# An edge-gated graph layer on one core: PSUM products copied by ScalarE and used by VectorE two steps later, aggregation in pairs

## The chip, the cores and the metric

The kernel runs on one core of a Trainium2 chip. The metric is the device time of one execution in microseconds. Before the change it is 1182.6 us, the median of three runs (1182.56 to 1185.6). The profiled execution that the tables below come from spans 1195.2 us.

The engines are called as the profile calls them: PE is TensorE (PEld are its weight loads), DVE is VectorE, ACT is ScalarE, POOL is GpSimd, SP is SyncE.

## The reference

There are 16 graphs (batch entries) of 1024 nodes with 256 features, and one sparse matrix `adj` (1024 x 1024) for all of them. For each edge u -> v a gate is computed from the features of both ends, and two sums over the edges go through two weight matrices:

```python
pre_u = einsum('bud,dk->buk', h_t, W1[:d])
pre_v = einsum('bvd,dk->bvk', h_t, W1[d:])
hidden = relu(pre_u[:, :, None, :] + pre_v[:, None, :, :] + b1)
S = sigmoid(einsum('buvk,ko->buvo', hidden, W2)[..., 0] + b2[0])
a_t = einsum('buv,bud->bvd', S * A_a, h_t)
m_t = einsum('uv,bud->bvd', A_m, h_t) * h_t
z_t = beta1 * h_t + beta2 * (einsum('bvd,de->bve', a_t, Wa) + ba) \
                  + beta3 * (einsum('bvd,de->bve', m_t, Wm) + bm)
```

Here `h_t` is `x`, and `A_a` and `A_m` are both `adj`. Some nine entries of a column of `adj` are not zero, so the kernel works on lists of edges.

## The kernel before

The work is cut into 32 blocks: 4 groups of 4 graphs times 8 tiles of 128 nodes v. A block has ten steps (`s` = 0 to 9), two windows of 64 nodes with five tiles of 128 edges each. A step `n` handles one edge tile:

- POOL gathers the tile's rows from a table in HBM by an indirect DMA: per edge 8 KB, namely `pre_u` of four graphs and `h` of four graphs (`fetched`, five buffers).
- PE expands `pre_v` to the edges with a 0/1 matrix (`expand`, into `pc` in PSUM, two buffers).
- VectorE adds the two into `t`, and for each graph does relu, multiplication by `W2` and the sum (`gate`); ScalarE makes the sigmoid `gt` from it and scales the aggregation's left operand `left`.
- PE sums the rows of `h` into the nodes (`aggregate`), in 32-column pieces.

The order of instructions on each engine is the order of the program text (a manual schedule). `after(step, f)` puts `f` into the instruction stream at a later step, in `do(step)`, which stands behind the gate of that step.

```python
def gate(n):
    t = one.tile([P, GB, D], FP, name="t")
    nc.vector.tensor_tensor(t, fetched[n % NF][:, :GD]..., pcs.pop(n)..., ALU.add)          # L539
    for b in range(GB):
        nc.vector.scalar_tensor_tensor(t[:, b, :], t[:, b, :], 0.0, w2_b,
                                       ALU.max, ALU.mult, accum_out=sc[:, b:b + 1])         # L543
    nc.scalar.activation(gt, sc, AF.Sigmoid, bias=b2_b)                                     # L546
    for b in range(GB):
        nc.scalar.activation(lefts[n][:, :m, b, 1, :], lefts[n][:, :m, b, 0, :], AF.Copy,
                             scale=gt[:, b:b + 1])                                          # L549
```

Beside the steps, three jobs of a block are spread over them. `halves` computes `pre_v` of the next block and splits it into a rounded part `X` and the rest `low`[...]. `turn_over` transposes the sums and multiplies one of them by `h`. `block_end` makes the two final products and adds `beta1 * h`:

```python
def halves(k):
    X = cuts[k] = big.tile([P, NW, GD], FR, name="X")
    low = one.tile([P, GD], FR, name="low")
    for h in range(2):
        step = yield
        ...                                                     # pre_v of two graphs, into p (PSUM "misc", two buffers)
        nc.scalar.copy(X[:, 0, c], p)                                                       # L418
        after(step + 1, lambda c=c, p=p: nc.vector.tensor_tensor(
            low[:, c], p, X[:, 0, c].bitcast(FP), ALU.subtract))                            # L419
    ...                                                         # ScalarE moves X and low to where the matmul wants them

def turn_over(k, w, q, step):
    ...                                                         # PE transposes, ScalarE copies into LT (L581)
    def times_h():
        nc.vector.tensor_tensor(m, m, hTs[order[k]]..., ALU.mult)                           # L591
    after(step + 1, times_h)

def block_end(k):
    for h in range(2):
        for bb in range(2):
            step = yield
            if bb == 0:
                pz = small("pz")
                add_row(pz, bias_p)
            for i, wt in enumerate((w_m, w_a)):
                ...                                             # two matmuls each (L608)
        def add(h=h, pz=pz):
            nc.vector.scalar_tensor_tensor(hb[:, 2 * h:2 * h + 2, :], hb[:, 2 * h:2 * h + 2, :], be1,
                                           pz..., ALU.mult, ALU.add)                        # L612
        after(step + 1, add)
    after(step + 2, lambda: nc.sync.dma_start(out[...], hb))
```

The main loop, cut to what matters:

```python
for n in range(total + 2):
    k, s = divmod(n, T)
    if 1 <= n <= total:
        aggregate(n - 1)                                        # L560
        fetch_val(2)
        if n - 1 + NF < total:
            fetch(n - 1 + NF)                                   # L453, into the buffer just used; NF = 5
        if n % TW in (0, MID + 1):
            half_end(n - 1, 0 if n % TW else 1)                 # ScalarE copies a finished sum out of PSUM
    if n < total:
        gate(n)
        ...
    do(n)
    if n + 2 < total:
        expand(n + 2)                                           # L523
    ...                                                         # pieces of halves, turn_over, block_end, tables
```

Blocks of the first two groups run while the tables of the later groups and the edge lists of the later node tiles are still being made (products with `w_u`, transfers of `hT` and `table`, and short VectorE work).

Of the kernel before, what the change touches and what calls it, by code (L numbers as in the profile page):

```python
# [7 lines left out]
FP = mybir.dt.float32  # L8
FR = mybir.dt.float32r
I32 = mybir.dt.int32  # L10
AF = mybir.ActivationFunctionType
ALU = mybir.AluOpType
AX = mybir.AxisListType
P = 128
# [3 lines left out]
def kernel(  # L18
# [42 lines left out]
    nc = tc.nc  # L61
    B, N, D = x.shape
    NT = N // P
    DC = D // P
    GB = 4
    NG = B // GB
    GD = GB * D
# [290 lines left out]
    def after(step, f):  # L358
        due.setdefault(step, []).append(f)
# [48 lines left out]

    def halves(k):
        X = cuts[k] = big.tile([P, NW, GD], FR, name="X")  # L410
        low = one.tile([P, GD], FR, name="low")
        for h in range(2):
            step = yield
            c = slice(2 * h * D, (2 * h + 2) * D)
            p = small("p")
            add_row(p, b1_p)
            half_product(p, hTs[order[k]], w_v, h, True)
            nc.scalar.copy(X[:, 0, c], p)  # L418
            after(step + 1, lambda c=c, p=p: nc.vector.tensor_tensor(  # L419
                low[:, c], p, X[:, 0, c].bitcast(FP), ALU.subtract))  # L420
        yield
        nc.scalar.copy(X[W:, 1, :], X[W:, 0, :].bitcast(FP))
        for w in range(NW):
            yield
            nc.scalar.copy(X[(1 - w) * W:(2 - w) * W, w, :], low[w * W:(w + 1) * W].bitcast(FP))

    engines = mybir.EngineType
    main.enter_context(tc.manual_schedule(
# [80 lines left out]

    marks, pcs, accs, evs, hbs, LTs, lefts = {}, {}, {}, {}, {}, {}, {}

    def load_mark(q):
# [12 lines left out]
    def left_adj(n):  # L527
        k, g, vt, w, j = where(n)
        i = vt * NW + w
        m = len(QUARTERS[j])  # L530
        o = max(2 * j - 1, 0)
        lefts[n] = wk.tile([P, 2, GB, 2, V], FP, name="left")
        nc.scalar.activation(lefts[n][:, :m, :, 0, :], onehot[:, i, o:o + m, :].unsqueeze(2).to_broadcast([P, m, GB, V]),  # L533
                             AF.Copy, scale=val[:, i, j:j + 1])

# [15 lines left out]
    def aggregate(n):  # L551
        k, g, vt, w, j = where(n)
        left, f = lefts.pop(n), fetched[n % NF]
        for i, q in enumerate(QUARTERS[j]):
            h, r = divmod(q, 2)
            first = j == h * MID and r == 0
            if first:
                accs[h] = psa.tile([P, 2, D], FP, name=f"acc{h}")
            for b in range(GB):
                nc.tensor.matmul(accs[h][b * 2 * V:(b + 1) * 2 * V, r, :],  # L560
                                 left[:, i, b].rearrange("p k v -> p (k v)"), f[:, GD + b * D:GD + (b + 1) * D],
                                 start=first, stop=(j == q + 1), skip_group_check=True)


    def half_end(n, q):

        evs[q] = one.tile([P, 2, D], FP, name=f"ev{q}")
        nc.scalar.copy(evs[q], accs.pop(q))  # L568

    def turn_over(k, w, q, step):  # L570
        if w == 0 and q == 0:
            LTs[k] = one.tile([P, DC, GB, 2, P], FP, name="LT")
        LT = LTs[k]
        pt = small("pt")
        ev = evs.pop(q)
        for i in range(4):
            r, c = divmod(i, DC)
            nc.tensor.transpose(pt[:, i * P:(i + 1) * P], ev[:, r, c * P:(c + 1) * P], ident)  # L578
        v = slice(w * W + q * U, w * W + (q + 1) * U)
        r = (w * W + q * U) // V  # L580
        nc.scalar.copy(LT.rearrange("p c b k (r v) -> p r (c b k) v", v=V)[:, r:r + 2],  # L581
                       pt.rearrange("p (r i v) -> p r i v", r=2, v=V))
        apart = k == BS - 1 and w == NW - 1
        if not apart:
            if not q:
                return
            v = slice(w * W, (w + 1) * W)

        def times_h():
            m = LT[:, :, :, 0, v]  # L590
            nc.vector.tensor_tensor(m, m, hTs[order[k]].rearrange("p b c n -> p c b n")[:, :, :, v], ALU.mult)  # L591
            if w == NW - 1 and q == 1:
                del hTs[order[k]]
        after(step + 1, times_h)

    def block_end(k):

        g, vt = order[k]
        hb = hbs[k]
        for h in range(2):  # L600
            for bb in range(2):
                step = yield
                if bb == 0:
                    pz = small("pz")
                    add_row(pz, bias_p)
                for i, wt in enumerate((w_m, w_a)):
                    for c in range(DC):
                        nc.tensor.matmul(pz[:, bb * D:(bb + 1) * D], LTs[k][:, c, 2 * h + bb, i, :], wt[:, c, :],  # L608
                                         start=False, stop=(i == 1 and c == DC - 1), skip_group_check=True)

            def add(h=h, pz=pz):
                nc.vector.scalar_tensor_tensor(hb[:, 2 * h:2 * h + 2, :], hb[:, 2 * h:2 * h + 2, :], be1,  # L612
                                               pz.rearrange("p (b d) -> p b d", b=2), ALU.mult, ALU.add)
            after(step + 1, add)
        after(step + 2, lambda: nc.sync.dma_start(
            out[g * GB:(g + 1) * GB, vt * P:(vt + 1) * P, :].rearrange("b p d -> p b d"), hb))
        del hbs[k], LTs[k]


# [64 lines left out]
    for n in range(total + 2):  # L684
        k, s = divmod(n, T)
        if 1 <= n <= total:
            aggregate(n - 1)
            fetch_val(2)
            if n - 1 + NF < total:
                fetch(n - 1 + NF)  # L690
            if n % TW in (0, MID + 1):
                half_end(n - 1, 0 if n % TW else 1)
        if n < total:
            gate(n)
            if n + 1 < total:
                left_adj(n + 1)
        if n % TW == 1 and n // TW + 1 < total // TW:
            load_mark(n // TW + 1)
# [3 lines that stand above are left out]
        if n == 1:  # L702
            w_a = load_weights(Wa, "w_a", nc.sync)
            w_m = load_weights(Wm, "w_m", nc.sync)
            bias = load_rows(bm, D, "bias", nc.sync)
            ba_b = load_rows(ba, D, "ba_b", nc.sync)
            be1 = load_rows(beta1, 1, "be1", nc.sync)
            be2 = load_rows(beta2, 1, "be2", nc.sync)
            be3 = load_rows(beta3, 1, "be3", nc.sync)
            after(10, scale_late)  # L710
        if s == 4 and k < BS:
            hbs[k] = big.tile([P, GB, D], FP, name="h_blk")
            if k < BS - 1:
                g, vt = order[k]
                nc.sync.dma_start(hbs[k], x_rows[vt * P:(vt + 1) * P, g * GB:(g + 1) * GB, :])
            else:
                for v, m, f in tails:
                    for h, o in tail_rows(x, v, m, f):
                        nc.sync.dma_start(h, o)
        for i in advance.get(n, ()):  # L720
            next(made[i], None)
        if (s == 1 and 0 < k < BS) or n == total:
            turn_over(k - 1, 1, 1, n)
        if s in (3, 4, 5, 6) and 0 < k < BS:
            if s == 3:
                end = block_end(k - 1)
                next(end)
            go(end, n)
        if s == 7 and k < BS:
            turn_over(k, 0, 0, n)  # L730
            turn_over(k, 0, 1, n)
        if s == 9 and k < BS:
            turn_over(k, 1, 0, n)
        if n == total - 2:
            end = tail(tails[:2], n)
            next(end)
        elif n == total - 1:
            go(end, n)
        elif n >= total:
            end = tail([tails[2 + n - total]], n)  # L740
            next(end)
            go(end, n)
            go(end, n)
        if k + 1 < BS and s in (0, 2, 3, 4, 6):
            if s == 0:
                parts = halves(k + 1)
                next(parts)
            go(parts, n)
        if n in loads:
            load_hT(loads[n])  # L750
            if loads[n] not in begun:
                copy_h(loads[n])
                begun.add(loads[n])
        if n in at:
            if at[n] != last:
                last = at[n]
                piece = rows(last)
                next(piece)
            go(piece, n)
        if n == 100:  # L760
            nc.gpsimd.partition_all_reduce(longest, rest, P, bass_isa.ReduceOp.max)
            after(n + 12, count_rest)
# [114 lines left out]
```

## Time and profile before

| | busy, us | share of the span |
|---|---|---|
| PE matmuls | 1097.9 | 92% |
| PE weight loads | 724.7 | 61% |
| VectorE | 1066.9 | 89% |
| ScalarE | 840.4 | 70% |
| GpSimd | 426.1 | 36% |
| DMA | 391.39 MB | mean 327 GB/s |

Shares of a whole span hide that this kernel has stages. How to read on: cut the span where the work changes (here by the starts of the `t` additions, one per step), ask for busy times and DMA share in each stage, then for the waits of the fullest engine there. A row of a wait reads "engine and line that waited <- what ended the wait: us in total, times, longest". A group row reads "line engine operation out<-in, shapes, count | busy us, mean ns of one | idle time before it, and what ended it". Two rows carry most of VectorE's time: the multiply-and-sum L543, 1280 of them at 422 ns, and the addition L539, 320 at 1215 ns.

### The profile page before, as it was taken

What the parts mean: (1) busy time and instruction counts of PE and PEld (TensorE: products, weight loads), DVE (VectorE), ACT (ScalarE), POOL (GpSimd) and SP (SyncE); (2) the same over time, 40 slices, a digit from 0 to 9 for tenths busy, and PEclk for the clock granted to TensorE, in tenths of its full rate; (3) what the DMA queues carried; (4) which work ended last, traced back from release to release, by engine and by line L of the source; (5) the groups of instructions that cost most, each with busy time, mean ns of one, the idle gap of its engine ahead of it and who ended that gap; (6) DMA issues with size and microseconds to landing.
All of it is one profiled execution on the core that took longest, in us unless ns stands there. A gap on an engine that the chain in (4) does not pass through costs nothing. (4 is left out here: it accounts for less than half of the span.)

```text
span 1195.2 us, 23788 instructions
## 1 busy us (share of the span) xinstructions
PE 1097.9 (92%) x7633; PEld 724.7 (61%) x7633; DVE 1066.9 (89%) x3515; ACT 840.4 (70%) x2498; POOL 426.1 (36%) x428
## 2 busy tenths in 40 slices
PE   7667988999889898999999999999999999999986
PEld 6544655666556565666666666666666666666653
DVE  8769879989988988899899999999999999999994
ACT  3346666677667665777777777787878777777873
POOL 1557652433263226333233333333333333333330
PEclk9968899999999999999999999999999999999998
DMA  9988889899979978999999999999999999999992
GB/s 279 312 307 261 258 319 333 315 336 377 320 254 373 361 244 302 357 384 360 351 329 379 359 331 371 362 356 386 358 367 345 356 324 326 326 341 328 335 340 76
DMA packets 147046, 391.39 MB, mean 327 GB/s; under 512 B 16752, under 2 KB 105328, under 8 KB 110704
## 3 DMA queue, kind: packets, MB, share of 16 engines
q0 software_dynamic: 50016, 300.50, 68.5%
q1 hardware_dynamic: 81616, 74.99, 19.6%
q10 hardware_dynamic: 15280, 14.29, 3.7%
q8 instruction: 63, 1.03, 0.3%
q14 instruction: 71, 0.58, 0.1%
HBM read 393.78 MB, written 50.33 MB: 372 GB/s over the span
## 5 line engine op out<-in xcount | busy, mean ns | idle before, releaser
L453 POOL DMA_INDIRECT fetched<-table,uidx x320 | 329.7, 1030 | 675.5 <-PE acc L560 509.6
L543 DVE SCALAR_TENSOR_TENSOR t<-t,w_b 128x256 f32<-128x256 f32 x1280 | 469.3, 422 | 20.1 <-ACT LT L581 0.5
L539 DVE TENSOR_TENSOR t<-fetched,pc 128x1024 f32<-128x1024 f32 x320 | 388.8, 1215 | 22.4 <-DMA fetched<-table,uidx 8.6
L560 PE MATMUL acc<-fetched,left 128*32 128x256 f32 x4096 | 334.2, 394 | 32.3 <-ACT left L549 16.8
L549 ACT ACTIVATE left<-left,gt 128x32 f32<-128x32 f32 (+1 forms) x1280 | 299.4, 304 | 10.4
L523 PE MATMUL pc<-X,mark 128*128 128x512 f32 x640 | 238.1, 454 | 21.1 <-DVE t L539 13.6
L560 PEld LDWEIGHTS acc<-fetched,left 128*32 128x32 f32 x4096 | 129.9, 110 | 177.2 <-issue 46.9
L546 ACT ACTIVATE gt<-sc,b_b 128x4 f32<-128x4 f32 x320 | 95.3, 298 | 140.5 <-DVE t L543 133.9
L523 PEld LDWEIGHTS pc<-X,mark 128*128 128x128 f32 x640 | 97.2, 191 | 156.6 <-issue 102.2
L608 PE MATMUL misc<-w_a,LT 128*128 128x256 f32 x496 | 127.3, 379 | 0.0
L608 PE MATMUL misc<-w_m,LT 128*128 128x256 f32 x496 | 127.1, 378 | 0.0
L384 PE MATMUL misc<-w_u,hT 128*128 128x256 f32 x448 | 109.2, 390 | 11.0 <-ACT few L298 3.6
L533 ACT ACTIVATE left<-onehot,val 128x128 f32<-128x128 bf16 (+1 forms) x320 | 116.5, 364 | 0.0
L384 PE MATMUL misc<-w_v,hT 128*128 128x256 f32 x448 | 107.9, 384 | 0.0
L543 DVE DVE_READ_ACCUMULATOR t<-t,w_b 128x1 f32 x1280 | 104.2, 81 | 0.0
L608 PEld LDWEIGHTS misc<-w_m,LT 128*128 128x128 f32 x496 | 93.7, 189 | 17.2
L384 PEld LDWEIGHTS misc<-w_u,hT 128*128 128x128 f32 x448 | 85.8, 195 | 27.3 <-issue 4.4
L608 PEld LDWEIGHTS misc<-w_a,LT 128*128 128x128 f32 x496 | 94.2, 190 | 12.8
L568 ACT COPY ev<-acc 128x512 f32<-128x512 f32 x128 | 75.1, 587 | 34.7 <-PE acc L560 26.8
L341 POOL DMA_INDIRECT val<-in_adjT_dram,vidx x80 | 83.6, 1046 | 33.4 <-issue 21.9
L384 PEld LDWEIGHTS misc<-w_v,hT 128*128 128x128 f32 x448 | 86.7, 194 | 14.3
L581 ACT COPY LT<-misc 128x512 f32<-128x512 f32 x128 | 71.1, 575 | 24.0 <-PE pc L523 12.0
(158 smaller groups left out, 830.9 us busy)
## 6 DMA issues: line engine op xcount, KB each, us to landing
h_blk<-in_x_dram SPq DMA_DIRECT2D x31, 512.0 KB
out_dram<-h_blk SPq DMA_DIRECT2D x31, 512.0 KB
hT<-in_xT_dram SPq DMA_DIRECT2D x28, 512.0 KB
table<-tab SPq DMA_DIRECT2D x26, 512.0 KB
table<-in_x_dram ACTq DMA_DIRECT2D x24, 512.0 KB
fetched<-table,uidx POOLq DMA_INDIRECT x320
table<-in_x_dram SPq DMA_DIRECT2D x8, 512.0 KB
table<-fetched SPq DMA_DIRECT2D x6, 512.0 KB
```

Source lines behind the costliest of these rows:

```text
L341: nc.gpsimd.indirect_dma_start(out=val[:, i, j:j + 1], out_offset=None, in_=adj_flat, in_offset=bass.IndirectOffsetOnAxis(ap=vidx[:, i, j: ...
L384: nc.tensor.matmul(p[:, bb * D:(bb + 1) * D], hT[:, 2 * h + bb, i, :], wt[:, i, :], start=(i == 0 and not begun), stop=(i == DC - 1), skip ...
L453: nc.gpsimd.indirect_dma_start(out=fetched[n % NF], out_offset=None, in_=table[g], in_offset=bass.IndirectOffsetOnAxis(ap=uidx[:, vt * NW ...
L523: nc.tensor.matmul(pcs[n][:, c], marks[n // TW][:, j * P:(j + 1) * P], cuts[k][:, w, c], start=True, stop=True)
L533: nc.scalar.activation(lefts[n][:, :m, :, 0, :], onehot[:, i, o:o + m, :].unsqueeze(2).to_broadcast([P, m, GB, V]), AF.Copy, scale=val[:, ...
L539: nc.vector.tensor_tensor(t, fetched[n % NF][:, :GD].rearrange("p (b d) -> p b d", b=GB), pcs.pop(n).rearrange("p (b d) -> p b d", b=GB), ...
L543: nc.vector.scalar_tensor_tensor(t[:, b, :], t[:, b, :], 0.0, w2_b, ALU.max, ALU.mult, accum_out=sc[:, b:b + 1])
L546: nc.scalar.activation(gt, sc, AF.Sigmoid, bias=b2_b)
L549: nc.scalar.activation(lefts[n][:, :m, b, 1, :], lefts[n][:, :m, b, 0, :], AF.Copy, scale=gt[:, b:b + 1])
L560: nc.tensor.matmul(accs[h][b * 2 * V:(b + 1) * 2 * V, r, :], left[:, i, b].rearrange("p k v -> p (k v)"), f[:, GD + b * D:GD + (b + 1) * D ...
L568: nc.scalar.copy(evs[q], accs.pop(q))
L608: nc.tensor.matmul(pz[:, bb * D:(bb + 1) * D], LTs[k][:, c, 2 * h + bb, i, :], wt[:, c, :], start=False, stop=(i == 1 and c == DC - 1), sk ...
```

## The change

ScalarE copies what VectorE used to read from PSUM: beside `X` now also the plain product into `low`, and the final product into a new tile `z`. VectorE then works in SBUF, on `low` once per block instead of twice, and one step later than before relative to PE's work. The aim is that VectorE never stands waiting for a product of PE or a copy of ScalarE that is only just being made. `turn_over`'s multiplication is moved one step later too; so that it may be, `block_end` does the product with `w_a` first and the one with `w_m`, which needs the multiplication, a step later. To make room, `h_blk` and `z` have one buffer each, and `h_blk` is loaded in step 0 of the following block.

Aggregation and refill are done in pairs in every even step: two tiles' aggregation one behind the other, each followed by its gather. `left` has four buffers instead of three for that.

```diff
 def halves(k):
-        low = one.tile([P, GD], FR, name="low")
+        low = one.tile([P, GD], FP, name="low")
...
             nc.scalar.copy(X[:, 0, c], p)
-            after(step + 1, lambda c=c, p=p: nc.vector.tensor_tensor(
-                low[:, c], p, X[:, 0, c].bitcast(FP), ALU.subtract))
+            nc.scalar.copy(low[:, c], p)
+        after(step + (2 if k else 1), lambda: nc.vector.tensor_tensor(low, low, X[:, 0, :].bitcast(FP), ALU.subtract))
...
-        lefts[n] = wk.tile([P, 2, GB, 2, V], FP, name="left")
+        lefts[n] = wk.tile([P, 2, GB, 2, V], FP, name="left", bufs=4)
...
-        after(step + 1, times_h)
+        after(step + (1 if k == BS - 1 else 2), times_h)

 def block_end(k):
+        z = big.tile([P, GB, D], FP, name="z", bufs=1)
         for h in range(2):
-            for bb in range(2):
+            for i, wt in ((1, w_a), (0, w_m)):
                 step = yield
-                if bb == 0:
+                if i:
                     pz = small("pz")
                     add_row(pz, bias_p)
-                for i, wt in enumerate((w_m, w_a)):
+                for bb in range(2):
...
-            def add(h=h, pz=pz):
-                nc.vector.scalar_tensor_tensor(hb[:, 2 * h:2 * h + 2, :], hb[:, 2 * h:2 * h + 2, :], be1,
-                                               pz.rearrange("p (b d) -> p b d", b=2), ALU.mult, ALU.add)
-            after(step + 1, add)
-        after(step + 2, lambda: nc.sync.dma_start(... hb))
+            sl = slice(2 * h, 2 * h + 2)
+            nc.scalar.copy(z[:, sl], pz.rearrange("p (b d) -> p b d", b=2))
+            after(step + 2, lambda sl=sl: nc.vector.scalar_tensor_tensor(z[:, sl], hb[:, sl], be1, z[:, sl],
+                                                                         ALU.mult, ALU.add))
+        after(step + 3, lambda: nc.sync.dma_start(... z))
...
         if 1 <= n <= total:
-            aggregate(n - 1)
             fetch_val(2)
-            if n - 1 + NF < total:
-                fetch(n - 1 + NF)
-            if n % TW in (0, MID + 1):
-                half_end(n - 1, 0 if n % TW else 1)
+        if 2 <= n <= total and n % 2 == 0:
+            for i in (n - 2, n - 1):
+                aggregate(i)
+                if i + NF < total:
+                    fetch(i + NF)
+            for i in (n - 2, n - 1):
+                if i % TW in (MID, TW - 1):
+                    half_end(i, 0 if i % TW == MID else 1)
...
-        if s == 4 and k < BS:
-            hbs[k] = big.tile([P, GB, D], FP, name="h_blk")
...                                            # the load of h_blk, and of the last block's rows
+        if s == 0 and 0 < k < BS:
+            hbs[k - 1] = big.tile([P, GB, D], FP, name="h_blk", bufs=1)
+            g, vt = order[k - 1]
+            nc.sync.dma_start(hbs[k - 1], x_rows[vt * P:(vt + 1) * P, g * GB:(g + 1) * GB, :])
+        if n == total - 6:
+            hbs[BS - 1] = hts.tile([P, GB, DC, P], FP, name="hT").rearrange("p b c n -> p b (c n)")
...
-        if k + 1 < BS and s in (0, 2, 3, 4, 6):
+        if k + 1 < BS and s in (0, 2, 3, 5, 6):    # when the pieces of halves are issued
```

More of the change, by code (lines that the diff above doesn't have):

```diff
@@ L424, in halves @@
             yield
-            nc.scalar.copy(X[(1 - w) * W:(2 - w) * W, w, :], low[w * W:(w + 1) * W].bitcast(FP))
+            nc.scalar.copy(X[(1 - w) * W:(2 - w) * W, w, :], low[w * W:(w + 1) * W])
     engines = mybir.EngineType
@@ L599, in block_end @@
         hb = hbs[k]
+        z = big.tile([P, GB, D], FP, name="z", bufs=1)
         for h in range(2):
-            for bb in range(2):
+            for i, wt in ((1, w_a), (0, w_m)):
                 step = yield
-                if bb == 0:
+                if i:
                     pz = small("pz")
                     add_row(pz, bias_p)
-                for i, wt in enumerate((w_m, w_a)):
+                for bb in range(2):
                     for c in range(DC):
                         nc.tensor.matmul(pz[:, bb * D:(bb + 1) * D], LTs[k][:, c, 2 * h + bb, i, :], wt[:, c, :],
-                                         start=False, stop=(i == 1 and c == DC - 1), skip_group_check=True)
-            def add(h=h, pz=pz):
-                nc.vector.scalar_tensor_tensor(hb[:, 2 * h:2 * h + 2, :], hb[:, 2 * h:2 * h + 2, :], be1,
-                                               pz.rearrange("p (b d) -> p b d", b=2), ALU.mult, ALU.add)
-            after(step + 1, add)
-        after(step + 2, lambda: nc.sync.dma_start(
-            out[g * GB:(g + 1) * GB, vt * P:(vt + 1) * P, :].rearrange("b p d -> p b d"), hb))
+                                         start=False, stop=(i == 0 and c == DC - 1), skip_group_check=True)
+            sl = slice(2 * h, 2 * h + 2)
+            nc.scalar.copy(z[:, sl], pz.rearrange("p (b d) -> p b d", b=2))
+            after(step + 2, lambda sl=sl: nc.vector.scalar_tensor_tensor(z[:, sl], hb[:, sl], be1, z[:, sl],
+                                                                         ALU.mult, ALU.add))
+        after(step + 3, lambda: nc.sync.dma_start(
+            out[g * GB:(g + 1) * GB, vt * P:(vt + 1) * P, :].rearrange("b p d -> p b d"), z))
         del hbs[k], LTs[k]
@@ L710 @@
             after(10, scale_late)
-        if s == 4 and k < BS:
-            hbs[k] = big.tile([P, GB, D], FP, name="h_blk")
[L713 to L719, printed above, removed]
+        if s == 0 and 0 < k < BS:
[4 more added lines that the diff above has]
+            hbs[BS - 1] = hts.tile([P, GB, DC, P], FP, name="hT").rearrange("p b c n -> p b (c n)")
+            for v, m, f in tails:
+                for h, o in tail_rows(x, v, m, f):
+                    nc.sync.dma_start(h, o)
         for i in advance.get(n, ()):
```

## The prediction

> **What bounds the kernel now.** I began with the busy row of the page: PE 92%, DVE (VectorE) 89%, DMA mostly 9 tenths in every slice. That average names no bound, so I cut the span into stages. The start of each `t` add (L539, one per step, 320 of them) gives the step times; ten steps are a block. Blocks 0 to 10 take about 39 us each (68 to 500 us), blocks 11 to 22 take 33.0 (500 to 896), and blocks 23 to 31 take 31.1 with hardly any spread (896 to 1177). The windows of the three stages:
>
> ```profile
> core 0: us, PE busy (x) PEld busy (x) DVE busy (x) ACT busy (x) POOL busy (x), PEclk, DMA share, GB/s
> 68.00:500.00 432.00, 387.73 (x2611) 256.45 (x2609) 379.92 (x1266) 289.82 (x859) 188.39 (x186) 0.95 0.89 311
> 500.00:896.00 396.00, 388.07 (x2778) 255.15 (x2774) 364.03 (x1156) 307.18 (x924) 124.50 (x121) 1.00 0.98 361
> 896.00:1177.00 281.00, 268.69 (x1946) 169.76 (x1944) 269.96 (x862) 216.52 (x670) 88.91 (x87) 1.00 0.92 328
> ```
>
> Columns: length, busy time of each engine, granted clock, DMA share, GB/s. Late, VectorE is busy 269.96 of 281 us: it is the bound there. In the middle the DMA engines are at 0.98 while VectorE has 32 us idle; early, nothing is full and VectorE has 52 us idle. So next I asked what VectorE waits for, stage by stage (early, then middle; us in total, times, longest):
>
> ```profile
> DVE low L419 <- ACT X L418: 12.8, 8, 4.4
> DVE h_blk L612 <- PE misc L608: 12.3, 9, 2.7
> DVE LT L591 <- ACT LT L581: 10.9, 7, 3.1
> ...
> DVE h_blk L612 <- PE misc L608: 8.0, 11, 1.3
> DVE t L539 <- DMA fetched<-table,uidx: 6.0, 11, 1.2
> DVE low L419 <- ACT X L418: 5.6, 6, 3.3
> ```
>
> Early 36.0 us and middle 13.6 us of VectorE's waits are at just the three operations that the change delays. Late, the same rows sum to 0.8 us. A third view, the groups of instructions, gives the costs (x count, then busy us, mean ns, idle before):
>
> ```profile
> L539 DVE TENSOR_TENSOR t<-fetched,pc 128x1024 f32<-128x1024 f32 x320 | 388.8, 1215 | 22.4 <-DMA fetched<-table,uidx 8.6 <-PE pc L523 3.4 <-DVE h_blk L612 0.8
> L612 DVE SCALAR_TENSOR_TENSOR h_blk<-h_blk,be,misc 128x512 f32<-128x512 f32 x62 | 46.1, 744 | 20.7 <-PE misc L608 20.6
> L419 DVE TENSOR_TENSOR low<-misc,X 128x512 fp32r<-128x512 f32 x64 | 43.9, 686 | 19.7 <-ACT X L418 19.7
> L591 DVE TENSOR_TENSOR LT<-LT,hT 128x512 f32<-128x512 f32 x55 | 37.8, 688 | 11.1 <-ACT LT L581 10.9
> L418 ACT CAST X<-misc 128x512 fp32r<-128x512 f32 x64 | 37.3, 583 | 38.4 <-PE misc L384 32.4 <-PE pc L523 4.0 <-PE misc L578 1.6
> ```
>
> Last, the refill loop. There are five `fetched` buffers, and POOL issues the next gather only when PE has aggregated the tile, as the waits of the whole run say. The timeline of one middle step shows PE's switch from aggregation to expansion:
>
> ```profile
> POOL fetched L453 <- PE acc L560: 509.6, 220, 6.7
> ...
> 703.18 0.16 PEld L560 LDWEIGHTS acc<-fetched,left 128*32 128x32 f32 x8 [0.17 <-issue]
> 703.18 0.64 PE L560 MATMUL acc<-fetched,left 128*32 128x256 f32 x8
> 703.75 0.30 PEld L523 LDWEIGHTS pc<-X,mark 128*128 128x128 f32 x2 [0.41 <-issue]
> ```
>
> The bracket is idle time: the weight load of `pc` stands 0.41 us after the last narrow load.
>
> From the trace I also took, for each gather, its issue, its landing (the last semaphore update of that DMA) and the add that uses it. Middle, medians: 8.25 us from issue to landing, 1.5 us from landing to use. Late: 7.5 and 2.6. The tightest tile is the one of step 1 of a block: it lands only 0.2 us (middle) and 0.45 us (late) before its add.
>
> [...] L612, which reads PSUM, takes 744 ns and L591, all in SBUF, 688; but L419 reads PSUM too and takes 686. [...] I read PE's 98% in the middle with the 64% of PEld (255.15 of 396) and don't call PE full. [...] gathers slow down while the output and `h_blk` transfers run.
>
> **The change, part by part.**
>
> *VectorE's own work.* A bare step lasts 2.80 us between adds. A late step with a half of `low` is 0.4 to 0.5 us longer (median), one with `h_blk` 0.5 to 0.6. So the two halves cost about 1.0 us per block; one 128x1024 subtraction streams twice the columns of a 512-wide one, so about 1.0 as well (2 x 0.5): nothing gained. The two `h_blk` operations become SBUF only[...]. **Sum: -2 us.**
>
> *VectorE's waits.* `low` runs two steps after ScalarE's second copy instead of one after PE's product, `z` two after its copy, `LT` two after. The longest wait at any of them was 4.4 us and a step is 3.1 to 3.9 us, so nearly all 36.0 + 13.6 us at these rows should be gone. Not all of it comes back as time: in such a pause PE, ScalarE and the DMA queues caught up, and in the middle DMA at 0.98 sets a limit near 33.0 x 0.98 = 32.3 us per block, if its rate stays. I credit 0.65 of the early waits (**-23 us**) and 0.6 of the middle ones (**-8 us**, which is 0.7 us x 12 blocks, just the room that DMA leaves). Late: 0.
>
> *ScalarE.* 64 copies of `low` and 62 of `z`, at the 583 ns of L418: 73 us more on an engine busy 840. In the late stage, 4 per block are 2.3 us on 24 (216.52 / 9 blocks) of 31.1: 26.4, or 85%. The heaviest step, 6, gets 4 left scalings (0.96), the next `left` (0.39), `mark` (0.71), `z` (0.58), the `low` cast (1.04) and the gate's 0.30: 4.0 us against a step of 2.9. It runs 1.1 us late and makes that up by step 8. Beside the path, but with little to spare.
>
> *PE.* The copy out of PSUM now comes from ScalarE within the step, so the two `misc` buffers come free earlier. In pairs the 0.41 us switch occurs 5 times per block, not 10: 2 us per block of weight-load idleness. As PE sets the end in no stage, this only shortens its lag.
>
> *The gathers.* This is the cost. Tile n-1 of a pair is aggregated as before. Tile n-2 was aggregated as soon as its gate was ready; now it stands behind the expansion and the products of the odd step. From PE's order, issue moves from about 5.4 to 6.6 us after use for step 0 (late), 5.8 to 8.5 for step 2, 6.0 to 8.0 for step 4, 6.4 to 7.6 for step 6. The slack of the gathers they start is 2.5, 3.4, 4.0 and 0.45 us. So the late stage has one deficit, at step 1, of about 0.7 us, and in the middle there are two or three of up to 1 us. The output transfer also moves one step later, onto the `h_blk` load: good for step 1, bad for steps 2 and 3. I put it at 0.5 us per block over 21 blocks: **+10 us.**
>
> Sum: -2 -23 -8 +10 = -23, so 1182.6 - 23 = **1160 us**.
>
> **Rivals.** (A) *The wait moves to DMA*: gathers issued late and two at a time leave the queues idle, and VectorE waits at L539 instead. For it: slack under half a microsecond at step 1, and 0.98 DMA share. Against: early slack is 2.5 us and more[...]. With 1.5 us per block over 21 blocks the time would be about 1182. (B) *ScalarE becomes the pace*: `z` and `low` wait in order for PE, then the gate's sigmoid behind them is late, then aggregation and refill. For it: step 6 and the 85%. Against: it already waits 38.4 us for PE at `X` with no harm to VectorE late. With 1 us on 32 blocks: 1190. (C) *The pauses were pure loss*: all 49.6 us come back and DMA keeps up (one block, 500 to 533 us, ran at 382 GB/s). Then 1135.
>
> **Range and chances.** C's 1135 and A's 1182 bracket my sum; I take 1137 to 1188. The 2% line is at 1159, almost my centre, so faster and same are near even. Slower by 2% needs B and A together: 0.05.
>
> **What would show it.** Right: VectorE's waits at `low`, `z` and `LT` under 5 us together; early blocks at 37 us; late blocks within 0.5 us of 31.1; ScalarE's busy time up by 73 us; the wait at L539 for gathers up from 8.6 to 15 or 20 us. The prediction is wrong if that wait passes 30 us, most of it in steps 1 to 3 (A); if VectorE is idle before PE's or ScalarE's rows of the gate chain (B); or if early blocks don't shorten though the waits are gone, which would mean that the pauses lay beside another limit.

## The result and the profile after

The changed kernel takes 1229.95 us (median of four runs, 1225.99 to 1231.27) against 1183.5 us before: ratio 1.0384, 95% interval 1.0354 to 1.0414. It is 46 us slower, and the prediction had said 1160.

The groups of VectorE's instructions, after (busy us, mean ns | idle time before it and what ended it), beside the two new copies on ScalarE:

```profile
L540 DVE TENSOR_TENSOR t<-fetched,pc 128x1024 f32<-128x1024 f32 x320 | 389.5, 1217 | 102.7 <-DMA fetched<-table,uidx 73.5 <-PE pc L524 8.0 <-PE misc L610 4.0
L614 DVE SCALAR_TENSOR_TENSOR z<-h_blk,be,z 128x512 f32<-128x512 f32 x62 | 46.3, 748 | 0.0
L420 DVE TENSOR_TENSOR low<-low,X 128x1024 f32<-128x1024 f32 x32 | 39.0, 1219 | 3.4 <-ACT low L419 3.4
L592 DVE TENSOR_TENSOR LT<-LT,hT 128x512 f32<-128x512 f32 x55 | 37.7, 686 | 0.0
L419 ACT COPY low<-misc 128x512 f32<-128x512 f32 x64 | 37.5, 586 | 0.0
L613 ACT COPY z<-misc 128x512 f32<-128x512 f32 x62 | 36.2, 584 | 31.7 <-PE misc L610 30.9
```

The change did what it was meant to do at the rows it touches: in front of these rows of `z`, `low` and `LT` VectorE is idle for 3.4 us in all, where it was 51.5. But the idle time before the `t` addition is now 102.7 us instead of 22.4, and 73.5 of it ends with the landing of a gather, instead of 8.6.

The windows of the same three stages, with the columns as in the prediction (their ends moved: the blocks 11 to 22 now end at 922 us), and VectorE's waits for gathers in the first two:

```profile
68.00:500.00 432.00, 378.77 (x2599) 263.44 (x2600) 379.36 (x1260) 312.04 (x904) 193.97 (x187) 0.93 0.88 311
500.00:920.00 420.00, 386.36 (x2764) 267.66 (x2763) 363.48 (x1138) 326.83 (x969) 127.72 (x120) 0.97 0.94 340
920.00:1177.00 257.00, 239.49 (x1740) 156.02 (x1738) 241.24 (x761) 211.62 (x635) 85.07 (x80) 1.00 0.89 325
```

```profile
DVE t L540 <- DMA fetched<-table,uidx: 31.5, 19, 5.0
...
DVE t L540 <- DMA fetched<-table,uidx: 36.2, 29, 5.9
```

In the middle the same VectorE work (363.48 us against 364.03) takes 24 us longer, and the DMA share falls from 0.98 to 0.94: the queues have less to do while VectorE waits for them. The experiments below show that this is not a rate limit: the gathers are asked for too late.

Taken by step, 43.7 of the 73.5 us are waited at the additions of step 1, and 67.9 at odd steps. With five buffers the tile of an odd step goes into the buffer of the even tile five steps before it, and the even tiles are those that pairing holds back.

The waits of the whole run show where the request comes from; the last line is the kernel before:

```profile
POOL fetched L453 <- PE acc L561: 547.2, 163, 10.0
PE pc L524 <- DVE t L540: 78.1, 62, 4.6
PE pc L523 <- DVE t L539: 13.6, 14, 2.1
```

POOL waits for PE's aggregation up to 10.0 us at a time (6.7 before). PE in turn stands 78.1 us before its expansion because VectorE hasn't done the addition that frees `pc` (13.6 before). A part of the longest middle block, of 41.7 us, shows the order, from the timeline (start, length, engine, instruction):

```profile
689.75 1.89 PE L384 MATMUL misc<-w_u,hT 128*128 128x256 f32 x8
...
691.28 0.81 PE L524 MATMUL pc<-X,mark 128*128 128x512 f32 x2
...
692.17 1.89 PE L610 MATMUL misc<-w_a,LT 128*128 128x256 f32 x8
...
693.99 1.93 PE L561 MATMUL acc<-fetched,left 128*32 128x256 f32 x32
...
695.37 1.09 POOL L453 DMA_INDIRECT fetched<-table,uidx  x1 [6.95 <-DVE t L540]
...
701.13 1.22 DVE L540 TENSOR_TENSOR t<-fetched,pc 128x1024 f32<-128x1024 f32 x1 [0.94 <-DMA fetched<-table,uidx]
```

The 32 matmuls at 693.99 are a pair: the tiles of steps 2 and 3. VectorE's addition for the first of them was at 683.9 us and the next addition at 686.8, so its gate was done by then. But in PE's queue it stands behind a `w_u` product, an expansion and the `w_a` product; of these the expansion and the `w_a` product (691.28 to 693.99) are what pairing put ahead of it. Its buffer is refilled at 695.37, 11.4 us after its use (the median of the tiles of step 2 in this stage is 10.4), and the gather that this issue starts lands at 701.0, just as VectorE needs it. The bracket of that issue names an addition whose end fell just there; the addition that read this buffer was long done, and what was still missing was the aggregation.

PE's granted clock, a share of its full speed, is lower than before too: 0.97 in the middle stage, where it was 1.00, and 0.88 in this block. In experiments 1 and 14, which don't hold the tiles back, it is 0.99 and 1.00 there. What the slower clock adds to the 46 us isn't separated by any run.

### The profile page after: what moved, and what is told of

Its sections match the earlier page's. It is cut to its first block, busy times and chain, and to the rows that moved or that the text cites. A ratio compares the mean times of both kernels' runs of the same rounds, so it can differ in the third digit from the quotient of the medians.

```text
span 1229.5 us, 23868 instructions
## 1 busy us (share of the span) xinstructions
PE 1088.2 (89%) x7633; PEld 749.5 (61%) x7633; DVE 1067.0 (87%) x3483; ACT 897.8 (73%) x2624; POOL 438.2 (36%) x428
## 3 DMA queue, kind: packets, MB, share of 16 engines
q8 instruction: 63, 1.03, 0.3%
## 5 line engine op out<-in xcount | busy, mean ns | idle before, releaser
L453 POOL DMA_INDIRECT fetched<-table,uidx x320 | 341.4, 1067 | 692.0 <-PE acc L561 547.2
L540 DVE TENSOR_TENSOR t<-fetched,pc 128x1024 f32<-128x1024 f32 x320 | 389.5, 1217 | 102.7 <-DMA fetched<-table,uidx 73.5
L561 PE MATMUL acc<-fetched,left 128*32 128x256 f32 x4096 | 321.0, 399 | 12.3 <-ACT left L550 10.5
L524 PE MATMUL pc<-X,mark 128*128 128x512 f32 x640 | 245.3, 466 | 84.1 <-DVE t L540 78.1
L550 ACT ACTIVATE left<-left,gt 128x32 f32<-128x32 f32 (+1 forms) x1280 | 299.3, 304 | 10.4
L561 PEld LDWEIGHTS acc<-fetched,left 128*32 128x32 f32 x4096 | 141.8, 112 | 152.3 <-ACT left L550 53.8
L524 PEld LDWEIGHTS pc<-X,mark 128*128 128x128 f32 x640 | 104.7, 194 | 189.2 <-DVE t L540 122.8
L384 PE MATMUL misc<-w_u,hT 128*128 128x256 f32 x448 | 112.9, 400 | 16.0 <-DMA hT<-in_xT_dram 5.3
L610 PE MATMUL misc<-w_a,LT 128*128 128x256 f32 x496 | 117.1, 379 | 0.0
L610 PE MATMUL misc<-w_m,LT 128*128 128x256 f32 x496 | 117.1, 379 | 0.0
L384 PEld LDWEIGHTS misc<-w_u,hT 128*128 128x128 f32 x448 | 88.6, 201 | 31.9 <-issue 5.7
L384 PE MATMUL misc<-w_v,hT 128*128 128x256 f32 x448 | 107.4, 383 | 0.0
L544 DVE DVE_READ_ACCUMULATOR t<-t,w_b 128x1 f32 x1280 | 104.3, 81 | 0.0
L384 PEld LDWEIGHTS misc<-w_v,hT 128*128 128x128 f32 x448 | 86.0, 192 | 14.0
L579 PE MATMUL misc<-ident,ev 128*128 128x128 f32 x512 | 79.2, 287 | 5.2 <-ACT LT L582 4.0
```

What stands on the lines that cost most here:

```text
L384: nc.tensor.matmul(p[:, bb * D:(bb + 1) * D], hT[:, 2 * h + bb, i, :], wt[:, i, :], start=(i == 0 and not begun), stop=(i == DC - 1), skip ...
L453: nc.gpsimd.indirect_dma_start(out=fetched[n % NF], out_offset=None, in_=table[g], in_offset=bass.IndirectOffsetOnAxis(ap=uidx[:, vt * NW ...
L524: nc.tensor.matmul(pcs[n][:, c], marks[n // TW][:, j * P:(j + 1) * P], cuts[k][:, w, c], start=True, stop=True)
L540: nc.vector.tensor_tensor(t, fetched[n % NF][:, :GD].rearrange("p (b d) -> p b d", b=GB), pcs.pop(n).rearrange("p (b d) -> p b d", b=GB), ...
L561: nc.tensor.matmul(accs[h][b * 2 * V:(b + 1) * 2 * V, r, :], left[:, i, b].rearrange("p k v -> p (k v)"), f[:, GD + b * D:GD + (b + 1) * D ...
```

## The experiments

They are numbered in the order in which they ran. A ratio is to the kernel before, timed on the same chip; chips differ by up to 1.5%.

**1. The later work without the pairs** (`lag_only`): the changed kernel with the old place of aggregation and refill.

```diff
-        if 2 <= n <= total and n % 2 == 0:
-            for i in (n - 2, n - 1): aggregate(i); fetch(i + NF) ...
+        if 1 <= n <= total:
+            aggregate(n - 1); fetch(n - 1 + NF) ...
```

> The changed kernel, but each tile is aggregated and its gather issued in the step after its gate, as before the change; the copies by ScalarE and the later VectorE work stay. Theory R (refill: pairing issues half of the gathers 2 to 4 us later, and VectorE waits for them): VectorE's waits at the t addition for a gather fall from 73.5 us to under 25 us, and the time to between 1150 and 1185 us. Rival S (the 126 added copies make ScalarE the pace, and gates and gathers follow late): the time stays above 1210 us, with most of the waits at the addition.

Measured: 1181.92 us, ratio 0.9975 (0.9952 to 0.9999). Waits for gathers at the addition are 36.0 us, half of what they were but not under 25. Rival S has fallen: the 126 copies are all there and the 48 us are gone.

**2. The pairs without the later work** (`pair_only`): the kernel before with the paired loop and four `left` buffers.

> The kernel before, with pairing alone (and left in four buffers): no added copies, no later VectorE work. Theory R: 1215 to 1245 us, waits at the t addition for gathers of 60 us and more. Rival S: within 1% of 1183 us, for ScalarE has no more work than before. If both parts cost, it lies between, near 1205 us.

Measured: 1249.11 us, ratio 1.0544 (1.0503 to 1.0584), a little outside what was expected. VectorE's waits have both kinds at once:

```profile
DVE t L539 <- DMA fetched<-table,uidx: 73.5, 58, 5.3
DVE h_blk L612 <- PE misc L608: 24.9, 15, 3.9
DVE low L419 <- ACT X L418: 15.6, 10, 3.6
DVE LT L591 <- ACT LT L581: 8.9, 6, 2.8
```

So pairing alone costs 64 to 66 us, and in its company the later work is worth 1.6% (1.0384 against 1.0544), where alone it is worth 0.25%.

**3. Pairs with the even tile let through early** (`even_early`): its aggregation and refill stand right behind the odd step's expansion, ahead of that step's products.

```diff
         if n + 2 < total:
             expand(n + 2)
+        if n % 2 and n < total:
+            aggregate(n - 1); fetch(n - 1 + NF)
```

> The changed kernel, but the even tile of each pair is aggregated at once behind the expansion of the odd step, ahead of that step's products and transposes, and its gather goes out there; the odd tile stays where it was. Theory R in the form that what stands between (products of the odd step) makes the delay: use to issue of even tiles falls back to 5.5 to 7 us from 8.5 to 10, and the time is within 1% of the kernel with single aggregation. If instead the wait of the expansion for VectorE's addition makes the delay, little changes: above 1215 us.

Measured: 1193.04 us, ratio 1.0079 (1.0042 to 1.0116), 0.9% above the kernel with single aggregation, as expected. From use to refill an even tile takes 7.8 us in the middle stage (median), against 9.3 in the changed kernel, 7.2 in `lag_only` and 6.7 before. That isn't quite the 5.5 to 7 expected, but it takes back three quarters of the loss: what holds the even tile is the odd step's products ahead of it in PE's queue, and only a little of it the expansion's own wait.

**4. Four buffers in the ring** (`ring4`): the kernel before, every gather one step later, nothing else.

```diff
-    NF = 5
+    NF = 4        # five tiles still allocated
```

> The kernel before with four gather buffers in the ring instead of five, so every gather is issued one step (2.8 to 3.9 us) later relative to its use, everything else alike. Theory R: slack was 1.5 to 4 us (medians of the stages), so waits at the t addition for gathers pass 150 us and the time passes 1300 us. If gathers are limited by the rate of the DMA engines and not by when they are issued, the time stays within 3% of 1183 us.

Measured: 1271.26 us (one run; the kernel before 1183.2), waits for gathers 104.3 us. A step of lead costs 7% and the pairs, which take 2.5 to 3.5 us from half of the gathers (`pair_only`, even tiles, medians of the stages), 5.4%. The 1300 us and the 150 us of waits were too much: in the middle stage a gather lands 7.6 us after its issue, where it was 8.2. Why it lands sooner isn't shown.

**5. The kernel before, profiled again** (`before_again`), without any edit.

> The kernel before, unchanged, profiled a second time: how much do the lengths of the three stages move from one profile to the next? The first profile spanned 1195.2 us beside a median of 1183. Every theory expects the late stage within 1 us of 250; if the early or the middle stage moves by more than 5 us, differences of that size between profiles say nothing.

Measured: stages of 431.7, 391.5 and 254.2 us, on a chip on which the kernel before has a median of 1200.4 us. The first profile had 431.5, 395.6 and 249.9. So the middle and the late stage each move by 4 us without any edit, the late one more than expected; chip and chance aren't separated. Stages are best compared on one chip.

**6. and 7. Six buffers**, with pairs and without (`pair_nf6`, `single_nf6`): the kernel before; the room comes from one buffer each less for `h_blk` and `tab`, and `h_blk` is loaded where the changed kernel loads it.

```diff
-    NF = 5
+    NF = 6
```

> The kernel before with pairing, and six gather buffers in the ring instead of five (room comes from one buffer less for h_blk and for tab, h_blk loaded in step 0 of the next block). Theory R (pairing costs because the refill comes too late for five buffers): the sixth buffer gives back a whole step of lead, so the waits at the t addition for gathers fall from 73.5 us to under 25 us and the time from 1249 to 1180 to 1200 us. Rival (pairing costs through PE's order itself, or through gathers that go out two at a time): still above 1225 us.

> The same six buffers with single aggregation. If lead still limits the kernel before (slack under half a microsecond at step 1): 1165 to 1178 us. If the DMA engines' rate limits the middle stage, a sixth buffer gives nothing there: 1178 to 1190 us, middle stage within 5 us of the one before, though the slack from landing to use is up by 2 us or more.

Measured on that slower chip: with pairs 1216.14 us, ratio 1.0115 (1.0075 to 1.0154); without 1197.98, ratio 0.9970 (0.9949 to 0.9991). The pairs' loss falls from 5.4% to 1.2%, and the gathers' wait to 0.5 us:

```profile
L539 DVE TENSOR_TENSOR t<-fetched,pc 128x1024 f32<-128x1024 f32 x320 | 389.4, 1217 | 21.5 <-PE pc L523 7.2 <-remote 3.0 <-DMA fetched<-table,uidx 0.5
```

This shows it from the other side: with the lead given back, pairing costs little. The 1.2% lies in the early stage, which takes 450.0 us with pairs and 435.3 without; what causes it there wasn't tested. Without pairs the sixth buffer raises the median slack of the middle stage from 1.4 us (`before_again`) to 4.6 and gains almost nothing: VectorE waits at `low`, `h_blk` and `LT` as before (20.5, 19.2 and 16.3 us).

**8. `h_blk` loaded far from the output** (`lag_spread`): as 1, with two `h_blk` buffers and the load in step 4; room from one buffer less for `tab` and for `left`.

```diff
-        if s == 0 and 0 < k < BS:      # h_blk of block k - 1, one buffer
+        if s == 4 and k < BS - 1:      # h_blk of block k, two buffers
```

> The changed kernel with single aggregation, and h_blk in two buffers again, loaded in step 4 of its own block, far from the output transfer, which in the changed kernel goes out together with that load at the end of step 8 (one tab buffer less makes room). Theory: the two 512 KB transfers together hold up the gathers of steps 2 and 3, where the slack fell from 2.1 and 1.7 us to 0.6 and 0.4 in the middle stage. Then the slack there rises above 1.2 us and the time falls from 1182 to between 1160 and 1175 us. Rival (the middle stage is limited by the DMA engines' rate, whatever the order): within 5 us of 1182.

Measured: 1202.19 us, ratio 1.0020 (0.9999 to 1.0040). No gain, against what was expected. The slack at steps 2 and 3 rose only from 0.6 and 0.2 to 1.1 and 0.7 us (the 0.4 of the expectation is 0.2 in the trace), and the middle stage, of 395.7 us, is not below the 391.5 of the kernel before on that chip. The total says less: the first `t` addition comes at 78.3 us, where the kernel of experiment 1 has 71.4; ScalarE waits 4.4 us for the only `tab` buffer before it, which it doesn't there. So nothing shows that the kernel of experiment 1 is held where the two transfers collide; with the late start a small gain isn't ruled out.

**9. Six buffers with the later work** (`lag_nf6`), room from `tab`, `left` and the small lists.

```diff
 # to the kernel of experiment 1
-    NF = 5
+    NF = 6
-    # in short: unread, few, L, tab, left: 1, 2, 2, 2, 4 buffers
+    # in short: unread in the buffer of t; few, L, tab: 1 buffer; left: 3
```

> Single aggregation, the copies by ScalarE and the later VectorE work of the changed kernel, and six gather buffers (room from one buffer each less for tab, the small lists and left). Theory L (the copies with later work remove some 50 us of VectorE's waits, and with five buffers these came back as waits for gathers issued too late): waits at low, z, LT and the t addition together under 20 us in the steps, ratio to the kernel before 0.96 to 0.98. Theory D (the DMA engines' rate bounds the middle stage whatever the lead): early stage shorter by some 20 us, middle not, ratio 0.975 to 0.99. Theory N (ScalarE's added work eats it): ratio 0.99 or more.

Measured: 1176.28 us, ratio 0.9956 (0.9938 to 0.9974): by the number, theory N. But its first `t` addition comes at 79.3 us, where the kernel of experiment 1 has 71.4; ScalarE waits 6.2 us for the only `few` buffer before it. Later VectorE's additions wait 12.0 us for ScalarE, which uses the buffer that `t` now shares with `unread`. These waits are new, so this run doesn't decide; 14 does.

**10. and 11. Half gathers** (`lag_half`, `after_half`): each gather brings only the `pre_u` half of its rows, 4 KB per edge, and the aggregation sums that half; the sum over `h` is left out.

```diff
-            out=fetched[n % NF], out_offset=None, in_=table[g],
+            out=fetched[n % NF][:, :GD], out_offset=None, in_=table[g],
```

> Single aggregation with the copies and the later work, five buffers, but each gather brings only the pre_u half of its rows (4 KB instead of 8 KB per edge), and the aggregation sums that half: the sum over h is left out. Theory D: the middle stage, 33 to 33.6 us per block, falls to VectorE's 31.1 to 31.4 of the late stage, and no wait for a gather is left. If PE or ScalarE bounds the middle stage instead, it stays at 33.

> The changed kernel, pairing included, with the same half gathers (sum over h left out). Theory R: gathers that land some 3 us sooner make up for the late issue, so the waits at the t addition fall from 73.5 to under 15 us and the time is within 1.5% of the half-gather kernel with single aggregation. If pairing costs by itself, by PE's order, it stays 30 us or more above that one.

Measured (one run each): 1160.73 us without pairs, 1176.26 with them. In the middle stage of the first the DMA share is 0.72, and the blocks still take 32.4 us (32.8 with whole gathers in 13), not the 31.1 to 31.4 of theory D: the DMA engines' rate isn't what keeps them above VectorE's pace. There VectorE waits for PE:

```profile
DVE t L540 <- PE pc L524: 9.5, 12, 1.9
DVE t L540 <- DMA fetched<-table,uidx: 3.0, 7, 0.5
```

With pairs the gathers, which in the middle stage now land 5.3 us after issue instead of 8.4, leave 30.5 us of waits (15 were expected), and pairing costs 1.3% instead of 4.1%.

**12. and 13. Before and the later work, profiled on one chip** (`before_c`, the kernel before, and `lag_c`, the kernel of experiment 1; no new edit).

> The kernel before, profiled on the same chip as the next three. Every theory: early stage (blocks 0 to 10) 425 to 435 us, middle (11 to 22) 390 to 396, late (23 to 30) 249 to 254.

> Single aggregation with the copies and the later work, profiled again beside the kernel before. If the gain of the early stage is real and only given back later: early 400 to 412 us, middle 396 or more, first t addition 2 to 3 us later. If the early 407 us of the first profile was chance: early above 422 us.

Measured: stages of 417.6, 392.8 and 252.2 us before and 407.0, 393.9 and 251.2 with the later work (1182.22 and 1173.96 us). The early gain is 10.6 us here, not 24, because the kernel before is itself 14 us quicker in its early stage than in the first profile, and quicker than the 425 to 435 expected. It is mostly kept: the middle stage is shorter than the 396 us or more expected, and these two single runs differ by 8 us, though the medians of experiment 1 show only 0.25%.

**14. Six buffers with the later work, the start mended** (`lag_six`): as 9, but the lists' `mark` shares the buffer of `key`, and one `RR` buffer is saved instead of those for `few`, `L` and `unread`.

```diff
 # to the kernel of experiment 1
-    NF = 5
+    NF = 6
-        mark = big.tile([P, E], FP, name="made", bufs=1)
+        mark = big.tile([P, N], FP, name="key", bufs=1)[:, :E]
-    # in short: RR, tab, left: 2, 2, 4 buffers
+    # in short: RR, tab: 1 buffer; left: 3
```

> As the six-buffer kernel with copies and later work, but the room comes from elsewhere (the mark of the lists shares the buffer of key, one buffer less for RR), so that the start isn't held up: there the first t addition came at 79.3 us, with 71.4 in the five-buffer kernel. Expected: first addition at 72 us, ratio to before 0.985 to 0.991, waits for gathers under 6 us, and the middle stage still at 390 us, with waits of the addition for PE's expansion.

Measured: 1160.08 us, ratio 0.9798 (0.9763 to 0.9832): the fastest of the kernels that do the whole work, 1.7 to 2.4% below the kernel before and better than expected, with ScalarE's 126 added copies in it. First addition at 69.8 us, stages of 398.4, 388.7 and 251.2. Its additions and its `z`, `low` and `LT`:

```profile
L540 DVE TENSOR_TENSOR t<-fetched,pc 128x1024 f32<-128x1024 f32 x320 | 389.2, 1216 | 32.5 <-PE pc L524 18.6 <-DMA fetched<-table,uidx 2.8
L614 DVE SCALAR_TENSOR_TENSOR z<-h_blk,be,z 128x512 f32<-128x512 f32 x62 | 46.3, 748 | 0.0
L420 DVE TENSOR_TENSOR low<-low,X 128x1024 f32<-128x1024 f32 x32 | 39.0, 1220 | 3.8 <-ACT low L419 3.6
L592 DVE TENSOR_TENSOR LT<-LT,hT 128x512 f32<-128x512 f32 x55 | 38.0, 691 | 0.7 <-ACT LT L582 0.7
```

Only 2.8 us are waited for gathers, and 4.5 us of idle time stand in front of these rows of `z`, `low` and `LT`: here both parts of the idle time are nearly gone together. What is left is mainly PE's expansion.

**15. The same with less for PE** (`six_lesspe`): half of the product with `w_m` is left out.

```diff
-                    for c in range(DC):
+                    for c in range(DC) if i else (DC - 1,):
```

> The same, with half of the product with w_m left out (8 of PE's weight loads and matmuls less per block, about 1.7 us). If PE bounds the middle stage: it falls from 32.5 us per block to VectorE's 31.3 to 31.6, DMA share stays near 1. If the DMA engines bound it: it stays at 32.3 or more, and waits for gathers come instead of those for PE.

Measured: 1152.98 us (one run). Middle blocks 12, 13 and 14 fall from 32.1, 32.7 and 32.7 to 31.3, 31.4 and 31.3 us, and blocks 18, 19, 21 and 22 from 31.4 to 32.0 down to 31.3 or 31.4 (block 17 goes from 31.5 to 32.2, and block 20 holds one stall of some 3.5 us). VectorE's pace is reached while the DMA share stays 0.97. Block 13 in 14 and in this kernel:

```profile
531.76:564.43 32.67, 32.62 (x233) 21.66 (x232) 30.25 (x96) 27.34 (x82) 10.82 (x11) 1.00 1.03 387
528.87:560.23 31.36, 30.86 (x228) 20.03 (x224) 30.21 (x97) 27.06 (x82) 10.14 (x10) 1.00 1.03 400
```

PE, busy for 32.62 of 32.67 us in the first, was the bound in those blocks. The stage as a whole falls only from 388.7 to 386.6 us. Blocks 15 and 16 hardly move (34.7 and 34.5, then 33.8 and 34.6); why is open. The granted clock, 1.00 in every middle block of 14, is 0.95 in these two now and 0.91 in block 20, whose stall, for PE, falls into a stretch at half clock (0.50 from 754.1 to 760.9 us).

## Why the prediction was wrong

**The step that failed is "The gathers".** It named the right mechanism, which the prediction also had as rival A, and even the right place, step 1. But it gave it 10 us; with the later work in place it costs 48 us (1229.95 less 1181.92), without it 66. Two things were mis-sized.

First, the delay. The prediction worked it out from the late stage, where PE has little backlog (POOL waits for its aggregation 2.6 us at a time at most, 6.3 in the middle), as 1.2 to 2.7 us. There it is right: the median from use to refill of even tiles went from 5.8 to 7.7 us, and the waits are 0.6 us per block, where 0.7 was predicted. But in the middle it went from 6.7 to 9.3, and in the early stage (from block 2 on) from 7.0 to 10.7, where PE's queue holds the table products as well. There the waits are 3.0 and 2.9 us per block.

Second, the sum. The prediction set each delay against the slack of its own tile and added up the deficits, 0.5 us per block for 21 blocks and none early. But the loop is closed: a late gather makes the addition late, the addition frees `pc` for PE's next expansion, and behind that expansion stands the next aggregation, which refills the next buffer. PE's waits for the addition, 78.1 us instead of 13.6, fit that loop; how much of the 48 us comes from it isn't measured. The early slack, from which the prediction took it that nothing would be lost there, fell from a median of 4.0 us to 0.84, and 31.5 us of the waits are early.

**"VectorE's waits", -31 us.** That they vanish was right (3.4 us left against "under 5"). The credit was not: alone they bring 0.25%, some 3 us. With five buffers a part of what VectorE no longer loses there it loses at gathers: 30.2 us in `lag_c` against 15.7 in `before_c`, and the refill comes later (7.2 us after use in the middle instead of 6.7). With a sixth buffer the same change takes the ratio from 0.997 (7) to 0.980 (14), some 20 us of the 31 credited. The mechanism was right, and what it needs, lead for the gathers, was missing. The sum itself was uncertain as well: three profiles of the kernel before have 36.0, 33.3 and 20.4 us of these waits early.

**The DMA limit of 32.3 us per block** by which the middle credit was cut does not exist: in experiment 15 blocks of 31.3 us ran, at shares of 0.98 to 1.03 and 367 to 400 GB/s. In the seven middle blocks named there PE was the bound, and with half gathers VectorE waits in the middle for PE. The prediction's remark that PE "sets the end in no stage" was wrong there.

**"VectorE's own work", -2 us**: 0.1 us more busy (1067.0 against 1066.9). The rows of `low` are 5 us shorter (39.0 against 43.9), but the engine's busy time is the same. Its pace tells more: a late block that waits for nothing takes 31.1 us before and 31.3 with the later work, in all of its kernels. That is 0.2 us more per block, by my estimate 6 us over 32 blocks, where 2 us less were predicted. The 2 us were the author's estimate, and `z` doesn't bear them out: all in SBUF it takes 748 ns where the form that read PSUM (L612) took 744. L612 and L591, which the prediction sets side by side (744 and 688 ns), are two different operations.

**"ScalarE"**: the copies take 73.7 us by their rows, as said; the engine's busy time rose by 57 and not by the 73 that were named as a sign, since rows of successive instructions overlap (see the end). Rival B is refuted by experiments 1 and 14. **"PE"**: after an aggregation the 0.41 us of idle weight loading shows 140 times instead of 229, and this brought nothing that could be seen. Why the gap is there stays open. Elsewhere weight loads do run under matmuls: in the timeline of the kernel before, L384's weight loads (1.72 us from 704.32) run under its own matmuls (1.89 us from 704.55), all of them with weights of 128 by 128.

Of the signs named, the wait for gathers passed 30 us, and 50.4 of its 73.5 us are in steps 1 to 3, as the prediction had said for rival A; the late blocks (31.3 to 33.2 us instead of within 0.5 of 31.1) and the early ones (39.0 on average instead of 37) came out wrong, for the reason above.

Rival A was sized at 1.5 us per block in 21 blocks. Measured were 3 us of gather waits per block in the first 23 and 0.6 in the last nine; the range's upper end and the 0.05 for slower rested on that size. (Two sums of the rivals are off by a few us, and nothing rests on it: B's comes to 1192, C's to 1131.)

## What to carry to other kernels

Before moving an operation that frees a buffer, take from the trace, for each transfer, the time from issue to landing and from landing to use: here 1.5 us of median slack, against an expected delay of 1 to 3 us, pointed to the answer. Take the delay in every stage and not in the calmest one, and don't add up the deficits of single tiles where the late user also delays the next refill. A wait that is removed brings time only if nothing else is as late: here the later work and the sixth buffer are worth 0.25% and 0.3% alone, and 2% together. Profile the kernel before more than once before crediting a wait that has a long tail; in this one three profiles had 36, 33 and 20 us.

## What the runs showed of the hardware

A DMA share of 0.98 was no limit. The middle stage ran at 361 GB/s and 33.0 us per block with a share of 0.98, and in experiment 15 at 369 GB/s, seven of twelve blocks at 31.3 or 31.4 us, with 0.97. In the kernel before an 8 KB packet of a gather takes 309 ns in the median, but 344 in the mean of the middle stage and 363 in the late one, where the load is lighter (328 GB/s instead of 361): part of the busy share is packets that take longer, not more bytes.

In the late stage of the kernel before a gather lands 7.8 us after its issue where an output or `h_blk` transfer is under way in that time, and 5.8 where none is (medians of 64 and 22 gathers).

Two ScalarE copies of 512 columns out of PSUM, back to back, start 0.48 us apart though each row reads 0.59 (689.95 and 690.43 us in the timeline of the changed kernel); rows summed overstate what they cost.

Less work for PE did not keep its granted clock up: in the middle stage it is 1.00 in experiment 14 and 0.98 in experiment 15, which has eight matmuls less per block (one profile each).
